# The third pass of a vision state-space, attention and FFN kernel: a list schedule, its residual stream spilled to DRAM, normalizations on ScalarE

## The chip, the cores and the metric

The kernel runs on one core of a Trainium2 chip. Time is device microseconds of one execution. Of the kernel before there are three runs: 10998.56, 11001.96 and 11004.07 us, median 11001.96. A separate execution was recorded by the hardware profiler; it took 11005.84 us, of which 11004.1 lie between its first and its last instruction (the span). Stages and lines below are of that execution.

The engines are PE (TensorE, the matmuls), DVE (VectorE), ACT (ScalarE), POOL (GpSimd) and SP, which here only issues DMA transfers. Each engine has a queue of its own and works it off strictly in the order in which the program was written down; an instruction whose inputs aren't ready holds up what stands behind it on that engine. PEld is PE's loading of weights.

## The reference

The input x is (8, 64, 64, 96) in f32: 8 images, 4096 tokens each, 96 channels. What is computed, cut to its core:

```python
# layer 0
x = x + L0_conv(gn(x))       # group norm, 96 -> 2 x 192 channels (xin, z), depthwise 3x3 conv, SiLU,
                             # a selective scan in four directions (16 states), y = their sum;
                             # y = layernorm_192(y) * gamma + beta; y = y * silu(z); out = y @ out_proj.T
# layer 1, per token t of 96 channels
t = t + L1_attn(ln_t(t))     # q, k, v = ln @ Wqkv + b, 6 heads of 16
                             # attn = q k^T * 16**-0.5 (no softmax), y = attn v, y @ Wff + bff
t = t + L1_ffn(ln_t(t))      # q_acc(q_mul(x) @ q_mul(W1).T + q_mul(b1)), relu, the same with W2: 96 -> 384 -> 96
# ln_t: (v - mean) / sqrt(var + 1e-5) over the 96 channels; q_mul rounds to 5 exponent and 2 mantissa bits
```

Attention without a softmax is linear: q (k^T v). So for one image it is enough to have the Gram matrix of its normalized tokens, 97x97 with a column of ones for the biases; from it follows one matrix of 97x96 that all the image's tokens are multiplied with.

## The kernel before

Three passes run one after the other over all images. The first makes the projections and the convolution, the second the scans, the third all that follows. The first two end at 9870 us of the profiled execution; the change leaves them as they are.

*The third pass.* An image is cut into 8 groups of 512 tokens (`UNITS`), a group into 4 blocks of 128 tokens (`NU`), tokens on the partitions. A **first half** (`first_part`) does this for one group: load y and yo, the sums of the two scan orientations, z and x (five transfers on SP); add y and yo on GpSimd; normalize y over its 192 channels; transpose it on PE into `pt` (two PSUM banks), scale and shift on ScalarE into `gt`; multiply with z on GpSimd; project on PE into `po`; add x on VectorE, which gives the residual stream `t`; normalize it into `ln`, with a column of ones; add its Gram matrix into `pg`, transpose it into `pl` and copy that to `lnT`. When 8 first halves of an image are done, `attention` makes the matrix `weff` out of `pg` in four small products. A **second half** (`second_part`) multiplies `lnT` with `weff` into `pa`, adds that to `t`, normalizes into `lf`, transposes (`pf`), rounds to 8-bit floats (`xq`), multiplies with W1 (three `ph`, copied to `h1` by ScalarE), adds the bias and clips on VectorE, rounds to `hq` on GpSimd, multiplies with W2 (`py`), copies to `y16`, adds the bias, adds to `t` on GpSimd and stores. With 8 images there are 64 first and 64 second halves; one of each is called a pair here.

*Normalizing.* `statistics` takes `bn_stats` and `bn_aggr` on VectorE and leaves mean and variance of 4 blocks in the small tile `mv`; `rstd_of` adds epsilon and raises to the power of -0.5 on GpSimd. Then y is normalized on ScalarE, after VectorE has made the bias -mean x rstd out of `mv` (`scalar_tensor_tensor`), and ln and lf on VectorE itself (`normalize`, one `tensor_scalar` per block):

```python
dve.tensor_scalar(dst[:, i, 0 : src.shape[2]], src[:, i, :], mv[:, i, 0:1], mv[:, i, 1:2], ALU.subtract, ALU.mult)
```

*Buffers.* `t` (12 KB a partition) and `lnT` (16 KB) hold a whole image each, in three buffers; what is loaded has five, most of the rest three or two. In PSUM there are three banks for transposes, two for products of 96 columns, two for `ph`, one for `pg`.

*The order.* Every half is a Python generator that yields between its steps. `take_turns` opens one unit in every second round, with at most 12 open, and in every round takes each open unit one step further. The list of units puts first halves of image b and second halves of image b-2 in alternation. So the order in which PE, VectorE, ScalarE and GpSimd find their instructions is that of the rounds, with no duration in it. `InOrder` keeps it on these four engines; the transfers on SP are ordered by the framework.

*The other way to order* is `weave`, which the first two passes use already. There a step yields an engine, a planned cost in us, a delay till its result can be used (0.3 where none is given), and if it needs a PSUM bank, that bank's `Slots`. `weave` keeps a planned time per engine and always writes down next the step that can begin earliest; among equals the one of smaller rank:

```python
begin = at[0] if len(at[5]) < 4 else max(at[0], at[5][3].when())
key = (max(begin, free.get(at[5][0], 0.0)), at[1])
if best is None or key < best[0]:
    best = key, at
```

A step that yields a name and numbers, such as `"weff", b`, waits for that event in the plan. `room` says how many units of a kind may be open at a time; the next opens when the one that many places before it has ended.

Of the kernel before, what the change touches and what calls it, by code (L numbers as in the profile page):

```python
# [33 lines left out]
F32 = mybir.dt.float32  # L34
F16 = mybir.dt.float16
BF16 = mybir.dt.bfloat16
F8 = mybir.dt.float8e5
AF = mybir.ActivationFunctionType
ALU = mybir.AluOpType
# [61 lines left out]
def vss_attn_ffn_kernel(ctx: ExitStack, tc: tile.TileContext, g: dict, out: bass.AP):  # L101
# [15 lines left out]

    b_d = [[dram.tile([2, NS, N, L], BF16, name=f"b_d{b}_{o}") for o in range(2)] for b in range(NB)]
# [6 lines left out]
    pass3(tc, g, ident, mhalf, engines, y_d, z_d, out)  # L125
# [705 lines left out]
def take_turns(units, every, at_most):  # L831

    active, rounds = [], 0
    units = iter(units)
    unit = next(units, None)
    while unit or active:
        if unit and rounds % every == 0 and len(active) < at_most:
            active.append(unit)
            unit = next(units, None)
        active = [u for u in active if next(u, "end") != "end"]  # L840
        rounds += 1


@with_exitstack
def pass3(ctx, tc, g, ident, mhalf, engines, y_d, z_d, out):
    nc = tc.nc
    pe, dve, act, pool = engines
    CA = C + 1
    wp = ctx.enter_context(tc.tile_pool(name="p3w", bufs=1))
    one = ctx.enter_context(tc.tile_pool(name="p3one", bufs=1))  # L850
    two = ctx.enter_context(tc.tile_pool(name="p3two", bufs=2))
    three = ctx.enter_context(tc.tile_pool(name="p3three", bufs=3))
    five = ctx.enter_context(tc.tile_pool(name="p3five", bufs=5))
    ps_tr = ctx.enter_context(tc.tile_pool(name="p3tr", bufs=3, space=PSUM))
    ps_mm = ctx.enter_context(tc.tile_pool(name="p3mm", bufs=2, space=PSUM))
# [40 lines left out]
    state = [{"units": 0} for _ in range(NB)]  # L896

    def statistics(src):

        st = three.tile([P, NU, 6], F32, name="st")  # L900
        mv = five.tile([P, NU, 2], F32, name="mv")
        for i in range(NU):
            dve.bn_stats(st[:, i, :], src[:, i, :])
        for i in range(NU):
            dve.bn_aggr(mv[:, i, :], st[:, i, :])
        return mv

    def rstd_of(mv):

        pool.tensor_scalar(mv[:, :, 1], mv[:, :, 1], 1e-5, None, ALU.add)  # L910
        pool.tensor_tensor(mv[:, :, 1], mv[:, :, 1], mhalf[:, 0:NU], ALU.pow)

    def normalize(dst, src, mv):
        for i in range(NU):
            dve.tensor_scalar(dst[:, i, 0 : src.shape[2]], src[:, i, :], mv[:, i, 0:1], mv[:, i, 1:2], ALU.subtract, ALU.mult)

    def tokens(src, q):
        return src[q * GRP : (q + 1) * GRP].rearrange("(n p) c -> p n c", p=P)

    def first_part(b, q):  # L920
        cols = slice(q * GRP, (q + 1) * GRP)
        if q == 0:
            state[b]["t"] = three.tile([P, NBLK, C], F32, name="t")
            state[b]["lnT"] = three.tile([CA, L], F32, name="lnT")
            state[b]["gram"] = ps_one.tile([CA, CA], F32, name="pg")
        t = state[b]["t"][:, NU * q : NU * (q + 1), :]
        lnT, pg = state[b]["lnT"][:, cols], state[b]["gram"]
        y, yo = (five.tile([P, NU, DI], F32, name=name) for name in ("y", "yo"))
        for o, dst in enumerate((y, yo)):
            nc.sync.dma_start(dst, tokens(y_d[b][o], q))  # L930
        zs = five.tile([P, 2, GRP], F32, name="zs")
        nc.sync.dma_start(zs[:, 0, :], z_d[b][0:P, cols])
        nc.sync.dma_start(zs[0 : DI - P, 1, :], z_d[b][P:DI, cols])
        xr = five.tile([P, NU, C], F32, name="xr")
        nc.sync.dma_start(xr, tokens(g["x"][b], q))
        for _ in range(3):
            yield
        pool.tensor_add(y, y, yo)
        yield
        mv = statistics(y)  # L940
        yield
        rstd_of(mv)
        yield

        dve.scalar_tensor_tensor(mv[:, :, 0], mv[:, :, 0], -1.0, mv[:, :, 1], ALU.mult, ALU.mult)
        yield
        for i in range(NU):
            act.activation(y[:, i, :], y[:, i, :], AF.Identity, bias=mv[:, i, 0:1], scale=mv[:, i, 1:2])
        yield
        pt = [ps_tr.tile([P, GRP], F32, name=f"pt{i}", tag="tr") for i in range(2)]  # L950
        for i in range(NU):
            blk = slice(i * P, (i + 1) * P)
            pe.transpose(pt[0][:, blk], y[:, i, 0:P], ident)
            pe.transpose(pt[1][0 : DI - P, blk], y[:, i, P:DI], ident)
        yield
        gt = three.tile([P, 2, GRP], F32, name="gt")
        for i, rows in enumerate((P, DI - P)):
            act.activation(gt[0:rows, i, :], pt[i][0:rows, :], AF.Identity, bias=gb[0:rows, i, 1:2], scale=gb[0:rows, i, 0:1])
        yield
        for i, rows in enumerate((P, DI - P)):  # L960
            pool.tensor_mul(gt[0:rows, i, :], gt[0:rows, i, :], zs[0:rows, i, :])
        yield
        po = ps_mm.tile([P, NU, C], F32, name="po", tag="mm")
# [4 lines left out]
        yield  # L968
        dve.tensor_add(t, po, xr)
        mv = statistics(t)  # L970
        yield
        rstd_of(mv)
        yield
        ln = three.tile([P, NU, CA], F32, name="ln")
        pool.memset(ln[:, :, C:CA], 1.0)
        normalize(ln, t, mv)
        yield
        pl = ps_tr.tile([P, GRP], F32, name="pl", tag="tr")
        for i in range(NU):
            at = NU * q + i  # L980
            pe.matmul(pg, ln[:, i, :], ln[:, i, :], start=at == 0, stop=at == NBLK - 1)
            pe.transpose(pl[0:CA, i * P : (i + 1) * P], ln[:, i, :], ident)
        yield
        act.copy(lnT, pl[0:CA, :])
        state[b]["units"] += 1

    def attention(b):

        def small(rows, lhsT, rhs, name):
            p = ps_mm.tile([P, NU, C], F32, name=f"ps_{name}", tag="mm")[0:rows, 0, :]  # L990
            pe.matmul(p, lhsT, rhs, start=True, stop=True)
            return p

        while state[b]["units"] < UNITS:
            yield
        yield
        gram = two.tile([CA, CA], F32, name="gram")
        dve.tensor_copy(gram, state[b]["gram"])
        yield
        p = small(CA, gram, w_kv[:, 1, :], "gv")  # L1000
        yield
        gv = two.tile([CA, C], F32, name="gv")
        dve.tensor_copy(gv, p)
        yield
        p = small(C, gv, w_kv[:, 0, :], "kvT")
        yield
        kvT = two.tile([C, C], F32, name="kvT")
        dve.tensor_mul(kvT, p, hmask)
        yield
        p = small(C, kvT, w_ff, "kvf")  # L1010
        yield
        kvf = two.tile([C, C], F32, name="kvf")
        dve.tensor_copy(kvf, p)
        yield
        p = small(CA, w_qT, kvf, "weff")
        yield
        weff = two.tile([CA, C], F32, name="weff")
        dve.tensor_copy(weff, p)
        dve.tensor_add(weff[C:CA, :], weff[C:CA, :], b_ff[C:CA, :])
        state[b]["weff"] = weff  # L1020

    def second_part(b, q):
        while "weff" not in state[b]:
            yield
        t = state[b]["t"][:, NU * q : NU * (q + 1), :]
        lnT = state[b]["lnT"]
        pa = ps_mm.tile([P, NU, C], F32, name="pa", tag="mm")
        for i in range(NU):
            blk = slice(q * GRP + i * P, q * GRP + (i + 1) * P)
            pe.matmul(pa[:, i, :], lnT[:, blk], state[b]["weff"], start=True, stop=True)  # L1030
        yield
        dve.tensor_add(t, t, pa)
        mv = statistics(t)
        yield
        rstd_of(mv)
        yield
        lf = three.tile([P, NU, C], F32, name="lf")
        normalize(lf, t, mv)
        yield

        pf = ps_tr.tile([P, GRP], F32, name="pf", tag="tr")
        for i in range(NU):
            pe.transpose(pf[0:C, i * P : (i + 1) * P], lf[:, i, :], ident)
        yield
        xq = two.tile([C, GRP], F8, name="xq")
        dve.tensor_copy(xq, pf[0:C, :], saturate=False)
        yield
        h1 = three.tile([P, NHC, GRP], F16, name="h1")
        for hc in range(NHC):
            ph = ps_mm.tile([P, GRP], F32, name="ph", tag="ph")  # L1050
            pe.matmul(ph, w1q[:, hc * P : (hc + 1) * P], xq, start=True, stop=True)
            act.copy(h1[:, hc, :], ph)
        yield
        for hc in range(NHC):
            dve.tensor_scalar(h1[:, hc, :], h1[:, hc, :], b1q[:, hc : hc + 1], 0.0, ALU.add, ALU.max)
        yield
        hq = two.tile([P, NHC, GRP], F8, name="hq")
        pool.tensor_copy(hq, h1, saturate=False)
        yield
        po = ps_mm.tile([P, NU, C], F32, name="py", tag="mm")  # L1060
# [3 lines left out]
        yield  # L1064
        y16 = two.tile([P, NU, C], F16, name="y16")
        act.copy(y16, po)
        yield
        dve.tensor_add(y16, y16, b2q.unsqueeze(1).to_broadcast([P, NU, C]))
        yield
        pool.tensor_add(t, t, y16)  # L1070
        nc.sync.dma_start(tokens(out[b], q), t)

    units = []
    for b in range(NB + 2):
        for q in range(UNITS):
            if b < NB:
                units.append(first_part(b, q))
            if b >= 2:
                units.append(second_part(b - 2, q))
        if b < NB:  # L1080
            units.append(attention(b))
    take_turns(units, 2, 12)
# [45 lines left out]
```

## Time and profile before

| | |
|---|---|
| median of 3 runs | 11001.96 us |
| the profiled execution | 11005.84 us, its span 11004.1 |
| last matmul of the second pass starts | 9866.5 us, 3.7 long |
| first GpSimd instruction of the third pass | 9893.0 us |
| first store of the output | 10052.2 us |
| last store of the output | 11000.9 us |
| busy in the whole span: PE, DVE, ACT, POOL | 7817.8, 9786.2, 9222.7, 9474.5 us |
| DMA: bytes, rate over the span | 2103.23 MB, 191 GB/s |

In a row of the profile a name stands for a tile with its buffer number left out, so `mv` is every such tile, and y and y16 are both `y`. "x256" counts instructions. Nearly all rows carry the line L91, the line of `InOrder` that records instructions, so they are told apart by their tiles. An f32 matmul is two records. A matmul's length in the profile is modelled, and matmuls overlap, so PE's busy time says little of how near it is to its peak. "Releaser" names what ended an engine's idle time; "issue" is time in which it waited for nothing that the profile shows.

### The profile page before, as it was taken

How to read it: one execution, taken by the hardware profiler on the slowest of the kernel's cores; microseconds unless marked ns; L12 is line 12 of the kernel's file. 1: busy time of each engine (PE TensorE's matmuls, PEld its weight loads, DVE VectorE, ACT ScalarE, POOL GpSimd, SP SyncE). 2: the span in 40 equal slices, each digit the busy share in tenths (PEclk: the TensorE clock that was granted, in tenths of full speed). 3: DMA queues.
4: the chain of work that ended last, by engine and by line, in shares of the span. 5: the costliest groups of instructions: out<-in, count | busy, mean ns of one | idle time of the engine just before them, and what ended most of it. 6: DMA issues, size and time to landing. Idle time of an engine off the chain costs nothing.

```text
span 11004.1 us, 151651 instructions
## 1 busy us (share of the span) xinstructions
PE 7817.8 (71%) x51232; PEld 6202.8 (56%) x51232; DVE 9786.2 (89%) x7286; ACT 9222.7 (84%) x21031; POOL 9474.5 (86%) x3366
## 2 busy tenths in 40 slices
PE   6874777777767777776677777776777777767667
PEld 2221656666556666665566666665666666556555
DVE  6671999999999999999999999999999999987777
ACT  4553999999999999999999999999999999973333
POOL 4563999999999999999999999999999999987555
PEclk8776999999899999989999999889999999887666
DMA  4554666669896666698966666989666668884331
GB/s 139 170 156 132 209 219 216 210 214 206 196 215 211 215 218 209 212 206 197 216 212 214 216 208 212 204 196 214 212 216 215 208 213 204 196 181 145 86 87 40
DMA packets 928011, 2103.23 MB, mean 191 GB/s; under 512 B 274392, under 2 KB 422649, under 8 KB 925701
## 3 DMA queue, kind: packets, MB, share of 16 engines
q1 hardware_dynamic: 927236, 2093.53, 67.6%
q8 instruction: 410, 6.72, 0.3%
q14 instruction: 365, 2.98, 0.1%
HBM read 1917.59 MB, written 175.66 MB: 190 GB/s over the span
## 4 chain that ended last, share of the span: by engine, by line
ACT 27%; DVE 21%; PE 17%; issue 17%; POOL 11%; DMA 2%; SPq 1%; DVEq 0%; POOLq 0%; ACTq 0%
DVE h L91 14%; ACT x L91 12%; ACT da L91 10%; POOL c L91 9%; PE wide L91 6%; PE acc L91 5%; DVE wide L91 3%; PE po L91 2%; DVE lf L91 2%; PE px L91 2%; ACT L91 1%; POOL xg L91 1%; PE pa L91 1%; ACT delta L91 1%; DVE ln L91 1%
## 5 line engine op out<-in xcount | busy, mean ns | idle before, releaser
L91 POOL TENSOR_TENSOR c<-c,h 128x2048 f32<-128x2048 f32 x1536 | 6965.3, 4547 | 394.8 <-DVE h L91 334.3
L91 DVE TENSOR_TENSOR_SCAN h<-da,carry,wide 128x1024 f32<-128x1024 f32 x2304 | 5253.1, 2330 | 199.6 <-PE wide L91 132.5
L91 ACT ACTIVATE x<-duT,bT 128x128 f32<-128x128 f32 (+1 forms) x14336 | 4154.9, 366 | 57.5 <-PE wide L91 51.2
L91 PE MATMUL acc<-ident,c 128*128 128x128 f32 x24576 | 3478.9, 297 | 548.6 <-POOL c L91 541.0
L91 ACT ACTIVATE da<-delta,a_neg 128x1024 f32<-128x1024 f32 x3072 | 3502.2, 1143 | 347.4 <-DVE h L91 336.5
L91 PEld LDWEIGHTS acc<-ident,c 128*128 128x128 f32 x24576 | 3129.5, 155 | 884.5 <-POOL c L91 750.9
L91 PE MATMUL wide<-ident,x 128*128 128x128 f32 x11264 | 1609.2, 291 | 874.1 <-DVE h L91 855.9
L91 PEld LDWEIGHTS wide<-ident,x 128*128 128x128 f32 x11264 | 1338.6, 149 | 1170.6 <-DVE h L91 512.5
L91 DVE TENSOR_TENSOR_SCAN h<-da,wide 128x1024 f32<-128x1024 f32 x768 | 1707.4, 2270 | 89.3 <-PE wide L91 61.1
L91 DVE TENSOR_TENSOR wide<-du,wide 128x1024 f32<-128x1024 f32 x1216 | 1458.7, 1211 | 335.0 <-DMA u<-u_d 224.1
L91 PE MATMUL wide<-xb,sel 96*128 96x512 bf16 x2432 | 751.7, 394 | 590.8 <-DVE h L91 495.2
L91 POOL TENSOR_TENSOR xg<-duT,bT 128x512 f32<-128x512 f32 (+1 forms) x640 | 890.9, 1406 | 77.5 <-PE wide L91 59.3
L91 PE MATMUL wide<-ident,xg 128*128 128x128 f32 x3584 | 503.4, 286 | 236.6 <-DVE h L91 231.2
L91 PEld LDWEIGHTS <-sel 96*128 96x128 bf16 x2432 | 222.9, 101 | 781.6 <-DVE h L91 387.6
L91 PEld LDWEIGHTS wide<-ident,xg 128*128 128x128 f32 x3584 | 415.2, 147 | 313.7 <-issue 147.2
L91 POOL TENSOR_TENSOR du<-delta,u 128x1024 f32<-128x1024 f32 x192 | 454.8, 2369 | 109.1 <-ACT delta L91 71.4
L91 ACT ACT_TABLE_LOAD x385 | 494.0, 1283 | 6.8
L91 PE MATMUL px<-u,w_xp 64*76 64x512 f32 (+1 forms) x512 | 402.6, 920 | 80.6 <-ACT xd L91 60.1
L91 DVE SCALAR_TENSOR_TENSOR u<-xpad,conv_w,u 128x3584 f32<-128x3584 f32 x96 | 423.6, 4413 | 1.6
L91 ACT ACTIVATE y<-y,mv 128x192 f32<-128x192 f32 x256 | 119.0, 536 | 338.3 <-DVE mv L91 294.6
L91 POOL TENSOR_TENSOR u<-u,term 128x512 f32<-128x512 f32 x96 | 286.7, 2986 | 130.7 <-ACT term L91 129.0
L91 POOL TENSOR_SCALAR mv<-mv 128x4 f32<-128x4 f32 x192 | 63.8, 332 | 382.5 <-DVE mv L91 381.7
(121 smaller groups left out, 6578.5 us busy)
## 6 DMA issues: line engine op xcount, KB each, us to landing
c<-xd_d SPq DMA_DIRECT2D x1024, 1024.0 KB
c<-xd_d SPq DMA_DIRECT2D x1024, 512.0 KB
u<-u_d SPq DMA_DIRECT2D x128, 512.0 KB
xdt<-dt_d SPq DMA_DIRECT2D x1152, 36.0 KB
xb<-b_d SPq DMA_DIRECT2D x384, 96.0 KB
u<-u_d SPq DMA_DIRECT2D x128, 256.0 KB
y_d<-y SPq DMA_DIRECT2D x24, 1024.0 KB
y<-y_d SPq DMA_DIRECT2D x64, 384.0 KB
```

The source lines that it names most:

```text
L91: ins = getattr(self.engine, op)(*args, **kwargs).ins
```

## The change

The third pass is written for `weave`; `take_turns` goes. Each step names its engine and a planned cost. At most 6 first halves, 1 attention and 6 second halves are open; the rank of a first half is 100 less than that of a second half of the same place, so among steps that can begin at the same time a first half's goes ahead.

`t` and `lnT` no longer stay in SBUF between the halves. A first half stores its 512 tokens of both in DRAM (`t_d`, `lnT_d`), and a second half loads them again. All tiles of the halves have six buffers. SP's transfers in this pass are held to the written order too.

All three normalizations go the way of y's: statistics on VectorE, power on GpSimd, bias on VectorE, and the last step on ScalarE. One of the three copies of `ph` to `h1` moves from ScalarE to VectorE. The two transposed halves of y take a bank each when they need it, and the Gram products of a group stand together ahead of its transposes. In the new queue of GpSimd 27 second halves have their last step before the last y plus yo, and 37 after it.

```diff
-    three = ctx.enter_context(tc.tile_pool(name="p3three", bufs=3))
-    five = ctx.enter_context(tc.tile_pool(name="p3five", bufs=5))
+    OPEN = 6
+    each = ctx.enter_context(tc.tile_pool(name="p3each", bufs=OPEN))
+    banks = {"tr": 3, "mm": 2, "ph": 2}
...
+    def standardize(src, dst, name, cost):
+        yield "dve", 4 * cost
         st = each.tile([P, NU, 6], F32, name=f"st{name}")
         mv = each.tile([P, NU, 2], F32, name=f"mv{name}")
...
+        yield "pool", 1.3
         pool.tensor_scalar(mv[:, :, 1], mv[:, :, 1], 1e-5, None, ALU.add)
         pool.tensor_tensor(mv[:, :, 1], mv[:, :, 1], mhalf[:, 0:NU], ALU.pow)
+        yield "dve", 0.15
+        dve.scalar_tensor_tensor(mv[:, :, 0], mv[:, :, 0], -1.0, mv[:, :, 1], ALU.mult, ALU.mult)
+        yield "act", 4 * cost
         for i in range(NU):
-            dve.tensor_scalar(dst[:, i, 0 : src.shape[2]], src[:, i, :], mv[:, i, 0:1], mv[:, i, 1:2], ALU.subtract, ALU.mult)
+            act.activation(dst[:, i, 0 : src.shape[2]], src[:, i, :], AF.Identity, bias=mv[:, i, 0:1], scale=mv[:, i, 1:2])
...
+        yield "pe", 3.8, 0.3, slots["mm"]
+        po, slot = take("mm", [P, NU, C])
...
+        end = yield "sp", 0.9, 3.0
+        sp.dma_start(tokens(t_d[b], q), t)
+        sp.dma_start(lnT_d[b][:, cols], lnT)
+        done["first", b, q] = end
...
     def second_part(b, q):
-        while "weff" not in state[b]:
-            yield
-        t = state[b]["t"][:, NU * q : NU * (q + 1), :]
-        lnT = state[b]["lnT"]
+        yield "first", b, q
+        yield "sp", 0.9, 3.0
+        t = each.tile([P, NU, C], F32, name="t2")
+        sp.dma_start(t, tokens(t_d[b], q))
+        lnT = each.tile([CA, GRP], F32, name="lnT2")
+        sp.dma_start(lnT, lnT_d[b][:, q * GRP : (q + 1) * GRP])
+        yield "weff", b
...
         for hc in range(NHC):
-            act.copy(h1[:, hc, :], ph)
+            end = yield ("act" if hc < 2 else "dve"), 0.6
+            (act.copy if hc < 2 else dve.tensor_copy)(h1[:, hc, :], ph)
...
-    take_turns(units, 2, 12)
+    for b in range(NB):
+        units += [("first", b * UNITS + q - 100, first_part(b, q)) for q in range(UNITS)]
+        units.append(("attention", 0, attention(b)))
+        units += [("second", b * UNITS + q, second_part(b, q)) for q in range(UNITS)]
+    weave(units, {"first": OPEN, "attention": 1, "second": OPEN}, done)
```

## The prediction

> **What bounds the kernel now.** I read the page's table of slices first, then busy time by stage, then the rows of the third pass, and last the order of time inside one of its periods. The change touches only the third pass, so the first question is how much that pass takes and how full its engines are. Slices of the page:
>
> ```profile
> DVE  6671999999999999999999999999999999987777
> POOL 4563999999999999999999999999999999987555
> PEclk8776999999899999989999999889999999887666
> ```
>
> Up to the 36th slice VectorE and GpSimd stand at nine tenths; after it both fall, and so does the clock. The last matmul of the second pass ends at 9870.2 us, the first instruction of the third pass on a compute engine other than weight casts (GpSimd, y plus yo) starts at 9893.0, the span ends at 11004.1. So the pass takes 1111 us after a gap of 23. The table of stages (columns: stretch, its length, busy us of PE, PEld, DVE, ACT, POOL with counts, clock, DMA share, GB/s):
>
> ```profile
> 9900.00:10000.00 100.00, 81.57 (x419) 65.84 (x417) 58.49 (x273) 46.84 (x89) 86.72 (x99) 0.70 0.72 210
> 10022.00:10898.00 876.00, 599.88 (x3091) 470.49 (x3091) 666.08 (x1969) 280.38 (x528) 514.65 (x579) 0.66 0.28 81
> 10898.00:11004.00 106.00, 74.87 (x455) 54.67 (x454) 90.38 (x283) 35.05 (x67) 62.54 (x64) 0.64 0.12 32
> ```
>
> At first only first halves run and GpSimd is 87% busy. In the 876 us in the middle, where a first and a second half alternate, nothing is full: VectorE 76%, PE 68%, GpSimd 59%. There the stores of the output lie 17.8 us apart (10052.2 to 10799.2, 42 intervals). At the end, second halves alone leave one per 5.95 us (10905.7 to 11000.9, 16 intervals). A first half among its like takes about 8 us even with the stalls of the start, so a pair costs more together than its halves apart. The next lines say why. Three are rows of groups (busy us, mean ns | idle us before); the fourth gives lf's shortest, median and longest ns; the last five are a stretch in order of time (start, length, and in brackets the idle time before):
>
> ```profile
> L91 DVE TENSOR_SCALAR lf<-t,mv 128x96 f32<-128x96 f32 x256 | 209.1, 879 | 1.4 <-POOL mv L91 1.3
> L91 DVE TENSOR_SCALAR ln<-t,mv 128x96 f32<-128x96 f32 x256 | 135.3, 590 | 9.7 <-POOL mv L91 9.4
> L91 DVE SCALAR_TENSOR_TENSOR mv<-mv 128x4 f32<-128x4 f32 x64 | 54.7, 855 | 4.8 <-POOL mv L91 4.8
> L91 DVE TENSOR_SCALAR lf<-t,mv x256: 291/325/4476, 10022.1 to 10990.1; 128x96 f32<-128x96 f32 x128
> ...
> 10503.91 6.28 DVE L91 TENSOR_SCALAR lf<-t,mv 128x96 f32<-128x96 f32 x4
> 10503.99 2.48 POOL L91 TENSOR_TENSOR gt<-gt,zs 128x512 f32<-128x512 f32 x2
> 10506.42 1.46 POOL L91 CAST hq<-h 128x1536 fp8e5<-128x1536 f16 x1
> 10507.84 1.79 POOL L91 TENSOR_TENSOR y<-y,yo 128x768 f32<-128x768 f32 x1
> 10509.76 0.64 PEld L91 LDWEIGHTS pf<-ident,lf 128*96 128x96 f32 x3 [4.27 <-DVE lf L91]
> ```
>
> A normalization instruction has a median of 325 ns but a mean of 879 (lf) and a longest of 4476: four of them take 6.28 us while GpSimd runs three kinds of work back to back, and PE waits 4.27 us for them. The chain of waits then alternates: DVE lf, PE po, DVE lf, PE po, through the whole pass. VectorE's 76% is thus partly standing still, and the written order puts PE's work behind it.
>
> [...] lf, ln and the two-input mv stretch, bn_stats with one input never does (240/243/263 ns shortest, median, longest). [...] the 4.4 us are longer than any one GpSimd instruction there, so back-to-back GpSimd work can keep VectorE out over several. [...] four pg and pl pairs took 2.3 us at the low clock and 1.15 at the high one; the mean clock of the pass is 0.66.
>
> **The change, part by part.** On every engine the instructions up to the end of the second pass stand in the same order, and the first loads of the third do too. So 9893.0 stays. Per pair of halves, 64 pairs:
>
> Removed from VectorE: lf and ln, (209.1 + 135.3)/64 = 5.4 us, of which some 2.5 is work (8 x 0.31) and 2.9 waiting. Added to it: two more mv of 0.15 (unblocked) to 0.86 (the mean of before); the third of the h1 copies, taken at 0.68 like the xq row of near size; together 1.0 to 2.4. VectorE's unblocked work is then 3.4 for a first half (bn_stats 1.86, bn_aggr 0.72, add 0.56, two mv 0.30) and 4.8 for a second (add 0.55, statistics 1.10, mv 0.15, xq 0.68, copy 0.68, three h1 1.05, y16 0.55): 8.2 a pair, 525 in all.
>
> Added to ScalarE: eight activations of 128x96. The rows of 128x64 (335 ns) and 128x128 (389) bracket them at 360: 2.9 us, less 0.59 for the h1 copy that leaves. ScalarE goes from 384/64 = 6.0 to 8.3 us a pair, 533 in all; it hides behind GpSimd. The normalization now goes VectorE, GpSimd, VectorE, ScalarE: one hop more, hidden by six open halves, and 0.5 us on the last unit only.
>
> GpSimd is unchanged: first half y 1.80, gt 2.54, two mv pairs 2.57, memset 0.13 = 7.04; second mv 1.29, hq 1.46, t 0.93 = 3.68. Together 10.7, 686 in all: the floor.
>
> PE's work is unchanged. From the first stage above: 419 records, 36 to a first half, so 11.6 halves in 81.6 us: 7.0 a half at clock 0.70. From the last: 74.9 us for 17.8 halves, 4.2 each.
>
> DMA: t and lnT are stored and loaded again, four transfers of 192 or 194 KB; a pair moves 2308 KB instead of 1536. SP issues 10 transfers a pair instead of 6, at 0.37 to 0.5 us each 4.5 us: hidden. Over some 820 us the 64 pairs make 151 MB, 184 GB/s; the stage of first halves already moved 210 at a DMA share of 0.72 with GpSimd fed. I take zero, covered by a pair's 10 to 13 us. Bound above: if the stage kept that 210, 720 us, still below my sum; late loads could add 100. A store of lnT waits for ScalarE, and behind it in SP's queue, now in written order, stand the loads for the half six later, some 60 us ahead: hidden.
>
> The order: in GpSimd's new queue 27 to 28 second halves stand among the 64 first halves, and about 36 follow the last. Stretch A, GpSimd: 64 x 7.04 + 28 x 3.68 = 554 us. At the 86.7% that the first-halves stage reached: 638. PE in it needs 64 x 7.0 + 28 x 4.2 = 566 at the clock of 0.70, VectorE 64 x 3.4 + 28 x 4.8 = 352 plus its blocks; three engines near each other, so I don't take more than 87%. Stretch B, 36 second halves: the 5.95 of before, less about 2.4 for lf (2.54, 1.86 and 2.80 in the tail), plus 0.68 and 0.5, gives 4.7; PE at the low clock needs 2.0 + 0.9 + 1.6 + 1.2 = 5.7. I take 5.2: 187. Draining the last half and its store, 10. Sum: 9893 + 638 + 187 + 10 = 10728 against the profiled span of 11004.1; the median of the runs is 2 us under that span, so **10726 us**, 2.5% faster.
>
> **Rivals.** *The order works better still.* The longer look-ahead fills GpSimd to 97% in A (571) and B runs at 4.7 (169): 10640. For it, the second pass, ordered by the same function, holds both engines at nine tenths; against it, PE's need beside a low clock. Chance 0.17.
>
> *Blocking or loads cost more.* A denser GpSimd blocks VectorE more often; seven instructions a pair (three mv, three h1, y16) can still be blocked. Means of before over their unblocked time: mv 0.70, lf 0.58, ln 0.28, h1 0.13, y16 0.03 us. At 0.75 each, VectorE needs 8.2 + 5.2 = 13.4 a pair, 64 x 13.4 = 860, with the same drain and some bubbles 10800 to 10900; late loads of t2 and lnT2 would give the same 10830. Chance 0.23.
>
> *Slower.* [...] VectorE in order stands behind each blocked mv, and ScalarE, PE and so GpSimd behind it. Before's period is 1111/64 = 17.36 us a pair. It decides from a mean wait of (17.36 - 8.2)/7 = 1.3 us per blockable instruction; with VectorE and GpSimd fully in turns, 8.2 + 10.7 = 18.9 a pair, the kernel ends near 9893 + 1210 = 11100. For it: single waits of 4.4 us exist already. Against it: the largest mean is 0.70, and a VectorE that lags starves GpSimd [...]. Chance 0.06, of which 0.01 falls within 0.2% of no change.
>
> *The list order does nothing:* the costs that it plans with are off (po is planned at 3.8 us and lasts 5.3 at the low clock, blocks at zero) and each queue's head waits, as in the turns. Only lf and ln's blocked 2.9 us a pair would be won at most, 186 us, and half given back to mv: about 10900 to 11000. Chance 0.04, of which 0.02 within 0.2%.
>
> **How the numbers follow.** My case, 10680 to 10800, has 0.50. Below it lies 0.17, above it 0.33. The range of 8 in 10 leaves out the best 0.08 and the worst 0.12: 10625 to 10905. A difference of under 0.2% (22 us) can hardly be told from no change. Faster by more: 0.92; within: 0.03; slower: 0.05.
>
> **What would show it.** Spans of the first two passes unchanged, first y plus yo at 9893. GpSimd at 80 to 90% from there for about 640 us, then 190 us of second halves at about 5.2 us apiece. No lf or ln on VectorE; 512 such activations on ScalarE of about 360 ns. The mean of mv on VectorE between 0.3 and 0.9 us; above 1.3 the slow rival holds. PE's clock in A above 0.70. DMA near 185 GB/s and no long waits for t2 or lnT2. I am wrong if the blocked instructions, or waits of GpSimd for PE or DMA, leave GpSimd under 75% in A.

## The result, and the profile after

The kernel after takes 11575.57 us (median of 4 runs, 11569.57 to 11581.51), the kernel before 11000.56 in the same comparison (4 runs, 10998.56 to 11004.07): ratio 1.0522, 95% interval 1.0504 to 1.0541. The change makes the kernel 575 us slower; the forecast was 10726. The profiled span is 11572.4 us. The first y plus yo of the third pass starts at 9894.4 us (9893.0 before), so everything was lost in the third pass: 1678 us instead of 1111.

The slices of the page after (same rows as shown of before, and the DMA share):

```profile
DVE  6663999999999999999999999999999999333334
POOL 4564999999999999999999999999999999444433
PEclk8766999998899999889999998999999989555555
DMA  4654666679976766889666678986666899433321
```

In the third pass the clock is down to five tenths, no engine but PE is half busy any more (PE, at that clock, 52% in A below), and the DMA engines, too, are mostly idle on average. No engine is full. The same by stretch, A from the first to the last y plus yo, B from there to the end (columns: stretch, its length, busy us of PE, PEld, DVE, ACT, POOL with counts, clock, DMA share, GB/s):

```profile
9893.00:11146.00 1253.00, 646.20 (x3112) 517.05 (x3112) 422.77 (x1726) 419.59 (x905) 534.32 (x618) 0.59 0.37 104
11146.00:11572.00 426.00, 181.71 (x984) 133.09 (x984) 169.35 (x566) 108.57 (x247) 144.32 (x150) 0.56 0.17 50
```

A lasts 1253 us where 638 were forecast, B with its draining 426 where 197 were. GpSimd does the 534 us of work in A that the sum of the prediction had put at 554, but is 43% busy with it instead of 87%. The waits of the third pass say what it waits for (us in total, times, longest), those of the compute engines:

```profile
POOL y L91 <- DMA yo<-y_d: 551.9, 53, 47.4
DVE sty L91 <- POOL y L91: 504.1, 48, 43.5
PEld mm L91 <- issue: 409.3, 334, 27.5
PE mm L91 <- DMA lnT<-lnT_d: 311.3, 41, 21.5
```

And those of SP's own queue in the same stretch:

```profile
SPq L91 <- DMA out<-t: 336.6, 57, 10.0
SPq L91 <- POOL t L91: 247.5, 35, 30.1
SPq L91 <- ACT lnT L91: 115.1, 15, 19.3
```

Transfers are late, although the rate is half of what it was in the first stage of before (104 against 210 GB/s). The place to look is where little else is under way, in B. One period of it in order of time (start, length; in brackets the idle time before and its releaser):

```profile
11438.02 1.99 PE L91 MATMUL mm<-weff,lnT 97*128 97x96 f32 x8 [7.93 <-DMA lnT<-lnT_d]
11438.74 0.36 SPq L91 DMA_DIRECT2D t<-t_d  x1
11439.15 0.35 SPq L91 DMA_DIRECT2D lnT<-lnT_d  x1
...
11444.39 0.38 SPq L91 DMA_DIRECT2D out<-t  x1
...
11449.41 1.57 PE L91 MATMUL mm<-weff,lnT 97*128 97x96 f32 x6 [4.83 <-DMA lnT<-lnT_d]
```

And the same period cut into short stretches, with the columns of the stages (the last two are the DMA share and GB/s):

```profile
11439.00:11441.00 2.00, 2.00 (x16) 1.72 (x16) 0.91 (x4) 0.52 (x1) 0.00 (x0) 0.50 0.41 104
11441.00:11442.50 1.50, 1.50 (x11) 0.96 (x8) 1.21 (x8) 0.55 (x2) 0.67 (x2) 0.54 0.10 26
11442.50:11444.20 1.70, 0.32 (x3) 0.11 (x2) 1.58 (x4) 0.00 (x0) 1.70 (x2) 1.00 0.06 25
11444.20:11446.00 1.80, 0.37 (x2) 0.00 (x0) 0.98 (x5) 1.39 (x4) 0.99 (x2) 0.94 0.43 126
11446.00:11447.50 1.50, 0.00 (x0) 0.00 (x0) 0.00 (x0) 1.50 (x6) 0.63 (x1) 0.50 0.07 27
11447.50:11449.20 1.70, 0.00 (x0) 0.00 (x0) 0.00 (x0) 1.16 (x4) 0.00 (x0) 0.50 0.07 25
```

A load of t and one of lnT, 192 and 194 KB, are issued within 0.5 us of each other. The load of t, and later the store of the output, show as short stretches at a share of 0.41 and 0.43. What remains for the rest of the time runs at a share of 0.06 to 0.07 and 25 to 27 GB/s: that is one of the sixteen DMA engines over which the page takes the mean (1/16 = 0.0625). The matmul that needs lnT starts 10.3 us after its load was issued. The packets in the trace agree: those of 2048 bytes, which in B are lnT's rows alone, follow one after the other, 84 ns each. 97 of them make 8.15 us; this load's took 8.05, since each starts 80 ns after the one before, with two short breaks. From 11280 to 11560 us exactly one was under way for 179 us, two for 9.

The store of the output that falls into this period shows what that does to a transfer that is spread. Of its 512 packets of 384 bytes, 480 ran from 11445.3 to 11446.1 us; the last 32, one sixteenth, began at 11448.97, right behind lnT's last packet, and were done at 11449.6. SP issued its next load at 11450.07.

lnT has 97 rows, 96 channels and the row of ones. Its packets went one by one (84 ns each, one every 80). Of the 512 packets of this load of t, four to a partition, up to 19 were under way at once, of those of the store up to 21. The measured share agrees: one engine works off lnT. That its 97 rows are the reason was the estimate to be tested.

From this the theory that the experiments test, called A: 64 stores and 64 loads of 97 rows take 128 x 8.15 = 1043 us of one engine, and every other transfer that is spread over all sixteen has a sixteenth of its bytes on that engine, and lands behind them. y and yo thus come late, and since SP issues strictly in order (all 5229 issues in the profile of after stand in the order of the program), so does what stands behind them. The rival B: it is the new queue of SP, where stores that wait for their data (247.5 and 115.1 us of SP's waits above) and loads of t2 that wait for a buffer (336.6) stand ahead of the loads of y, and six buffers of t2 and lnT2 are too few.

### The profile page after: what moved, and what is told of

Read it like the earlier page. It is cut to its first block, busy times and chain, and to the rows that moved or that the text cites. A ratio compares the mean times of both kernels' runs of the same rounds, so it can differ in the third digit from the quotient of the medians.

```text
span 11572.4 us, 152227 instructions
## 1 busy us (share of the span) xinstructions
PE 7870.1 (68%) x51232; PEld 6247.1 (54%) x51232; DVE 9545.3 (82%) x6966; ACT 9387.9 (81%) x21479; POOL 9471.1 (82%) x3366
## 4 chain that ended last, share of the span: by engine, by line
ACT 25%; DVE 17%; issue 16%; PE 14%; POOL 12%; DMA 8%; SPq 3%; DVEq 0%; POOLq 0%; ACTq 0%
DVE h L91 13%; ACT x L91 12%; ACT da L91 9%; POOL c L91 8%; PE wide L91 5%; PE acc L91 5%; DVE wide L91 3%; SPq L91 3%; DMA yo<-y_d 3%; PE mm L91 2%; DMA out<-t 2%; DMA lnT<-lnT_d 2%; PE px L91 1%; ACT L91 1%; POOL xg L91 1%
## 5 line engine op out<-in xcount | busy, mean ns | idle before, releaser
L91 POOL TENSOR_TENSOR y<-y,yo 128x768 f32<-128x768 f32 x64 | 115.4, 1804 | 607.0 <-DMA yo<-y_d 551.9
L91 DVE BATCH_NORM_STATS2 sty<-y 128x6 f32<-128x192 f32 x256 | 72.9, 348 | 576.3 <-POOL y L91 504.1
L91 ACT ACTIVATE y<-y,mvy 128x192 f32<-128x192 f32 x256 | 119.1, 539 | 371.8 <-DVE mvy L91 308.9
```

Source lines behind the costliest of these rows:

```text
L91: ins = getattr(self.engine, op)(*args, **kwargs).ins
```

## Experiments

All times are medians, beside runs of the kernel before on the same chip; ratios are to those, with 95% intervals.

**1. lnT as 96 rows and 1 row** (`e1_rows96`), otherwise the kernel after, the same for the load:

```diff
-        sp.dma_start(lnT_d[b][:, cols], lnT)
+        for rows in (slice(0, C), slice(C, CA)):
+            sp.dma_start(lnT_d[b][rows, cols], lnT[rows])
```

> The changed kernel, with each of the 128 transfers of lnT (97 rows of 2 KB) issued as two, 96 rows and 1 row; the same bytes, 128 more issues on SP. Theory A (a transfer of 97 rows is worked off by a single one of the 16 DMA engines, 97 packets of 84 ns one after the other = 8.15 us, 128 of them = 1043 us on that engine, and every other transfer has a share that stands behind them): 96 rows spread, about 0.5 us each, and the time falls to what was forecast for the change, 10650 to 10850 us. Theory B (SP's written order: the load of t2 waits for the output's store out of the same buffer to land, the store waits for GpSimd, and loads of y stand behind): nothing of that is touched, 11450 to 11650 us.

Measured 10857.34 us, ratio 0.9863 (0.9848 to 0.9877), 7 us above theory A's range and some 600 below theory B's. The same bytes in twice as many transfers take off 718 us. The waits of its third pass, the two lines that answer to those above:

```profile
POOL y L91 <- DMA yo<-y_d: 89.1, 26, 16.2
...
PE mm L91 <- DMA lnT<-lnT_d: 33.1, 21, 4.2
```

551.9 became 89.1, 311.3 became 33.1. SP's waits for its stores' data have not gone (POOL t 205.6, ACT lnT 175.2), only those for the landing of the output shrank, to 126.6. A holds: what is left of B in SP's queue can't be the main cause.

**2. More buffers instead** (`e2_more_buffers`): the kernel after, t2 and lnT2 with eight buffers, paid for by four of h1 and lf.

```diff
-        t = each.tile([P, NU, C], F32, name="t2")
+        t = more.tile([P, NU, C], F32, name="t2")
-        lnT = each.tile([CA, GRP], F32, name="lnT2")
+        lnT = more.tile([CA, GRP], F32, name="lnT2")
-        lf = each.tile([P, NU, C], F32, name="lf")
+        lf = less.tile([P, NU, C], F32, name="lf")
-        h1 = each.tile([P, NHC, GRP], F16, name="h1")
+        h1 = less.tile([P, NHC, GRP], F16, name="h1")
```

> The changed kernel with 8 instead of 6 buffers for t2 and lnT2 (and, to make room, 4 instead of 6 for h1 and lf), so that a load of t2 on SP waits for the landing of a store two halves further back. 97-row transfers stay. Theory A: the one DMA engine still needs 1043 us for lnT and some 64 x 6 = 390 us for its share of the rest, 1430 us from 9893 on: not under 11330 us, and I expect 11400 to 11570. Theory B: the 337 us that SP waits for stores to land go, and most of the loss with them: 10800 to 11200 us.

Measured 11452.87, ratio 1.0404 (1.0389 to 1.042), inside theory A's range. SP's waits for the landing of the output are no longer among its largest, and yet GpSimd waits as before:

```profile
POOL y L91 <- DMA yo<-y_d: 538.3, 56, 39.7
```

The buffers, less what the four of h1 and lf may cost, are worth 123 us beside the slow transfers; the 575 us they don't explain.

**3 and 4. The 97 rows in the kernel before** (`e3_before_97`, `e4_before_96`): two more stores of lnT per first half into DRAM that nobody reads, once with all 97 rows, once with 96. Nothing waits for them but the buffer.

The first:

```diff
         act.copy(lnT, pl[0:CA, :])
+        for i in range(2):
+            nc.sync.dma_start(lnT_d[b][i][:, cols], lnT)
```

The second:

```diff
         act.copy(lnT, pl[0:CA, :])
+        for i in range(2):
+            nc.sync.dma_start(lnT_d[b][i][0:C, cols], lnT[0:C])
```

> The kernel before with two more stores of lnT (97 rows of 2 KB) to DRAM in each first half, which nobody reads: the disputed transfers by themselves, 128 of them, on a kernel that has its own order and no spill otherwise. Theory A: the one engine needs 16.3 us a first half for them and about 4.7 for its share of the rest, 21 us against a period of 17.4 and of 8 where first halves run alone: 11200 to 11400 us. Theory B: 24.8 MB more in 1111 us and two issues of 0.4 us on an SP that is mostly idle: 10990 to 11030 us.

> As the run with 97 rows on the kernel before, but the two stores of each first half take only the first 96 rows of lnT (the row of ones is left out; nobody reads either). Theory A: 6 rows to each of 16 engines, 1 us a first half together: 10990 to 11030 us. If the number of bytes or of issues is what costs, it is as slow as the one with 97 rows.

Measured 11259.19, ratio 1.0225 (1.0208 to 1.0242), with 97 rows, and 11007.77, ratio 1.0005 (0.9996 to 1.0013), with 96. One row more costs 251 us; 128 stores of 192 KB cost nothing that can be measured. The first stage of the third pass with 97 rows:

```profile
9900.00:10000.00 100.00, 57.18 (x263) 46.58 (x264) 33.83 (x177) 27.48 (x52) 54.42 (x62) 0.59 0.46 129
```

And with 96 rows:

```profile
9900.00:10000.00 100.00, 83.07 (x438) 66.70 (x438) 58.98 (x281) 47.87 (x92) 87.95 (x101) 0.75 0.80 230
```

With more bytes than before (230 GB/s instead of 210) GpSimd is as busy as before, 88%. With 97 rows it falls to 54%, in the old order and with no spilled tile to be loaded. This is the effect of the slow transfers alone.

**5 and 6. What each part is worth once that is out of the way.** `e5_before_act`: the kernel before, its turns kept, only ln and lf normalized on ScalarE. `e6_rows96_dve`: the kernel of experiment 1 with ln and lf back on VectorE, so the list order, the spill and the moved copy of h1 without the normalizations.

The first of the two:

```diff
     def normalize(dst, src, mv):
+        dve.scalar_tensor_tensor(mv[:, :, 0], mv[:, :, 0], -1.0, mv[:, :, 1], ALU.mult, ALU.mult)
-            dve.tensor_scalar(dst[:, i, 0 : src.shape[2]], src[:, i, :], mv[:, i, 0:1], mv[:, i, 1:2], ALU.subtract, ALU.mult)
+            act.activation(dst[:, i, 0 : src.shape[2]], src[:, i, :], AF.Identity, bias=mv[:, i, 0:1], scale=mv[:, i, 1:2])
```

The second:

```diff
         pool.tensor_tensor(mv[:, :, 1], mv[:, :, 1], mhalf[:, 0:NU], ALU.pow)
+        if name != "y":
+            yield "dve", 1.1
+            for i in range(NU):
+                dve.tensor_scalar(dst[:, i, 0 : src.shape[2]], src[:, i, :], mv[:, i, 0:1], mv[:, i, 1:2], ALU.subtract, ALU.mult)
+            return
```

> The kernel before with one part of the change alone: ln and lf normalized on ScalarE (with a bias made on VectorE), everything else, the turns too, as before. Theory P (the blocked normalizations on VectorE set the period): the 4 to 6 us that lf holds up PE and VectorE in each 17.8 us go, 10700 to 10900 us. Theory Q ([...] each mv instruction stands right behind GpSimd's power in time, finds GpSimd at its next work, and waits as lf did): 10950 to 11050 us.

> The changed kernel with lnT moved as 96 and 1 rows, and ln and lf back on VectorE (planned at 1.1 us each), y still on ScalarE: what the move of the normalizations is worth within the new order. Theory P: VectorE gets 5 to 8 us a pair back, blocked time included, and becomes the bound: 10930 to 11050 us. Theory Q: [...] 10830 to 10900 us, near the 10857 of that kernel with them on ScalarE.

Measured 10855.13, ratio 0.9865 (0.985 to 0.9879), and 10921.92, ratio 0.9926 (0.9912 to 0.9941). The first lies in theory P's range; the second lies between the two ranges, 22 us above Q's and 8 below P's. The normalizations alone bring 149 us, as much as experiment 1 (146). Order, spill and moved copy alone bring some 80; with the normalizations there, they add nothing in the form of experiment 1 (10857.34 against 10855.13). The two gains don't add up. The rows of the moved instruction in the third pass of the first of the two:

```profile
L91 ACT ACTIVATE ln<-t,mv 128x96 f32<-128x96 f32 x256 | 98.5, 460 | 33.9 <-DVE mv L91 33.9
L91 ACT ACTIVATE lf<-t,mv 128x96 f32<-128x96 f32 x256 | 98.2, 460 | 30.0 <-DVE mv L91 30.0
```

**7 and 8. SP's queue after all, as a second-order cost.** `e7_rows96_more`: experiments 1 and 2 together. `e8_rows96_act_stores`: experiment 1 with the stores of t and lnT issued by ScalarE, where they hold up no load. The diff of the second:

```diff
-        end = yield "sp", 0.9, 3.0
-        sp.dma_start(tokens(t_d[b], q), t)
+        end = yield "act", 0.3, 3.0
+        act.dma_start(tokens(t_d[b], q), t)
         for rows in (slice(0, C), slice(C, CA)):
-            sp.dma_start(lnT_d[b][rows, cols], lnT[rows])
+            act.dma_start(lnT_d[b][rows, cols], lnT[rows])
```

> The changed kernel with lnT moved as 96 and 1 rows and 8 buffers for t2 and lnT2 (4 for h1 and lf): what SP's waits for the landing of output stores (127 us in 55 waits with 6 buffers) still cost. If they delay loads that engines wait for (GpSimd 89 us for yo, PE 33 us for lnT): 10770 to 10830 us. If SP's waits are slack: 10840 to 10875 us.

> The changed kernel with lnT moved as 96 and 1 rows and the stores of t and lnT issued by ScalarE right behind its copy of lnT, instead of by SP, so that no load stands behind SP's wait for that copy (175 us in 28 waits). If these waits delay loads that engines wait for: 10760 to 10830 us. If they are slack, or ScalarE's three issues a half cost as much: 10840 to 10900 us.

Measured 10815.39, ratio 0.9828 (0.9813 to 0.9842), and 10870.55, ratio 0.9878 (0.9862 to 0.9895). The buffers are worth 42 us, and SP's waits for the landing of the output are no longer among its largest. Taking the stores of t and lnT off SP brought nothing (13 us more, the intervals overlap); whether SP's waits for lnT, 175 us in sum, are slack, or ScalarE's own issues took back what they cost, no run separates. So B exists, but small: 42 us here and 123 in experiment 2, against 718 for A.

**9 to 11. The 130 us between experiment 1 and the forecast.** In its first 700 us PE is 81% busy at a clock of 0.69, GpSimd 74%:

```profile
9900.00:10600.00 700.00, 565.76 (x2948) 457.09 (x2948) 428.46 (x1656) 399.31 (x868) 517.32 (x600) 0.69 0.64 174
```

`e10_one_product` leaves out the second of the two products into po (so the last 64 of 192 channels are not projected), `e11_no_gate` leaves out the product with z on GpSimd; both are the kernel of experiment 1 otherwise. `e12_measured_costs` takes experiment 7 and plans with the durations that its rows show. Without the product:

```diff
-            pe.matmul(po[:, i, :], gt[:, 0, blk], w_out0, start=True, stop=False)
-            pe.matmul(po[:, i, :], gt[0 : DI - P, 1, blk], w_out1, start=False, stop=True)
+            pe.matmul(po[:, i, :], gt[:, 0, blk], w_out0, start=True, stop=True)
```

Without the gate:

```diff
             yield "pool", 1.3
-            pool.tensor_mul(gt[0:rows, i, :], gt[0:rows, i, :], zs[0:rows, i, :])
```

With measured costs, two of some fifteen:

```diff
-        yield "pe", 3.8, 0.3, slots["mm"]
+        yield "pe", 5.6, 0.3, slots["mm"]
...
-        yield "dve", 0.15
+        yield "dve", 0.7
```

> The kernel after with lnT moved as 96 + 1 rows, and the second of the two products of a block into po (the last 64 of the 192 channels) left out: 8 of 16 records of PE for each first half, the rest and its order unchanged. At the mean of 0.38 us a record in its rows that is 64 x 8 x 0.38 = 195 us of PE work less. Theory E (PE at its low clock is what fills the time while first halves run: 82 to 89% busy there, GpSimd 69 to 80%): at least half of it comes off 10857, 10660 to 10760. Theory G (GpSimd remains the bound, PE only waits along with it): 10820 to 10860. Theory L (neither; late landings and the order in the queues set the pace): 10820 to 10860.

> The kernel after with lnT moved as 96 + 1 rows, and the product of gt with zs left out (GpSimd, 2.54 us for each first half, 163 us in all; zs is still loaded and not read). Theory G (GpSimd is the bound while first halves run): 10690 to 10750. Theory E (PE is): 10800 to 10860, since GpSimd had 20 to 30% to spare. Theory L: 10800 to 10860 too; it is told from E by the run with one product left out.

> The kernel after with lnT moved as 96 + 1 rows, eight buffers for t2 and lnT2 and four for h1 and lf (10815), and the planned costs of the third pass set to the durations that its rows show: po 5.6 instead of 3.8, pt 1.4 instead of 0.6, pg 2.5 instead of 1.6, pl and pf 1.35 instead of 0.7, pa 2.6 instead of 1.3, py 2.0 instead of 1.0, mv 0.7 instead of 0.15, statistics and activations up by a seventh to a quarter. If an order made from wrong costs is what keeps the kernel from the forecast of 10726: 10700 to 10770. If PE's work at the low clock is the bound whatever the order: 10790 to 10840.

Measured 10819.37 (0.9827, 0.9812 to 0.9842) without the product, 10807.0 (0.982, 0.9805 to 0.9835) without the gate, 11023.9 (1.0018, 1.0011 to 1.0024) with measured costs. PE's busy time fell by 168 us (755 to 588 from 9900 on) and brought 38; GpSimd's fell by 162 (676 to 514) and brought 50. Theory E had asked for 10660 to 10760 without the product, theory G for 10690 to 10750 without the gate: neither engine is the bound by itself. Two stages of the run without the product show GpSimd full in one and starved in another, while PE has time to spare in both:

```profile
10200.00:10300.00 100.00, 60.31 (x432) 53.57 (x432) 78.16 (x285) 68.92 (x154) 89.07 (x105) 0.77 0.69 188
...
10400.00:10500.00 100.00, 59.78 (x359) 45.57 (x360) 57.64 (x212) 47.96 (x106) 64.63 (x71) 0.65 0.56 154
```

The miss is the run with measured costs: truer costs make the order worse by 209 us, against both expectations. Its stretch A lasts 922 us where experiment 7 has 720 (first to last y plus yo), for the same number of second halves to within two; GpSimd waits for yo 165.0 us instead of 66.6. In the order that these costs give, the loads are late again. Why wasn't settled; what the run shows is how much the order hangs on the planned numbers.

**12. Planning the landing later** (`e13_landing`): experiment 7, and the data of the two loads of a half planned to be there 9 us after the issue instead of 3.

```diff
-        yield "sp", 2.4, 3.0
+        yield "sp", 2.4, 9.0
...
-        yield "sp", 0.9, 3.0
+        yield "sp", 0.9, 9.0
```

> The kernel after with lnT moved as 96 + 1 rows, eight buffers for t2 and lnT2 and four for h1 and lf (10815), and one planned number changed at the two loads: their data is planned to be there 9 us after the issue instead of 3. Theory L (what is left of the forecast lies in loads that the written order uses too early; GpSimd waits 66.6 us for yo there): the waits for yo shrink to under 35 us and the time to 10700 to 10790. Theory E+G (PE and GpSimd hold each other up at 84 to 90% and 72 to 83%, whatever the loads do): 10800 to 10840. If the order gets worse by being planned anew, as with the durations of the rows: above 10840.

Measured 10795.0 us, ratio 0.9817 (0.9801 to 0.9834), the lowest median of this study. The wait of GpSimd for yo in experiment 7:

```profile
POOL y L91 <- DMA yo<-y_d: 66.6, 24, 10.7
```

With the landing planned later:

```profile
POOL y L91 <- DMA yo<-y_d: 21.1, 8, 6.0
```

The wait shrinks as expected; the time lies between the two expectations. The gain is not sure: it is 20 us between the medians, but the kernel before beside this run took 10994.81 instead of 11003.86, and the ratio's interval overlaps that of experiment 7. In the profiled executions the third pass, from its first y plus yo on, lasts 900 us instead of 928. Late loads were at most a small part of the rest.

## Why the prediction was wrong

**The step that failed is the DMA term**: "I take zero, covered by a pair's 10 to 13 us. Bound above: if the stage kept that 210, 720 us, still below my sum; late loads could add 100." It was worked out as bytes by rate. Neither bytes nor rate were the problem: experiment 1 moves the same bytes, at 174 GB/s in its first 700 us. What counts is how a transfer is spread: 97 rows stand on one engine for some 8 us, where a sixteenth of 194 KB per engine would be some six rows, 0.5 us at 84 ns a packet (an estimate). The term measured 718 us (11575.57 less 10857.34) in place of 0 to 100. The row count stood in the diff, `[CA, GRP]` with CA = 97. The third pass of before moves no such tile, but its first pass held a warning: 128 stores of xd with 76 rows of 2 KB. While these run, from 213 to 933 us, exactly four packets of 2 KB were under way for 144 us, longer than any other number but none. One such store that stands alone, at 224.4 us, took 2.1 us and had four of its 76 packets under way at once for 1.4 us of them, never more than five.

**The second failing step is the lead of the loads**: "behind it in SP's queue ... stand the loads for the half six later, some 60 us ahead: hidden". They were never that far ahead, with or without the 97 rows. From the issue of yo's load to the y plus yo that reads it, the median over the 64 halves is 78.7 us in before, 10.8 after (longest 11.9) and 6.3 in experiment 1 (longest 11.6). In the chain of work that ended last (start, length) such a load looks like this after:

```profile
10509.48 10.40 DMA yo<-y_d
```

And in experiment 1:

```profile
10558.47 6.24 DMA yo<-y_d
```

Six open halves are thus no look-ahead of six halves for the loads. The runs show two things that shorten the lead: `weave` was told that a load needs 3 us (told 9, experiment 12, the median is 10.9), and stores stand ahead on SP (issued by ScalarE, experiment 8, it is 10.3). So there was little to hide a late transfer behind. How much of the 718 us lies in this short lead, and how much in the second halves that wait for lnT itself, no run separates; in the kernel before, where no engine waits for what they write, 128 such stores cost 251.

The late landings come on top. SP itself was held up in y's own issues, a median of 3.0 us each (ns shortest, median, longest; y and yo are the first transfers of a half):

```profile
L91 SPq DMA_DIRECT2D y<-y_d x63: 367/3019/8424, 9897.2 to 11129.5; - x63
```

In the third pass of before the same row reads:

```profile
L930 SPq DMA_DIRECT2D y<-y_d x63: 359/360/1485, 9895.8 to 10794.5; - x63
```

With 96 and 1 rows the median is 377 ns. There the short lead costs less, but it isn't hidden either: GpSimd still waits 89.1 us for yo (experiment 1).

**What held** (figures of the run after). 9893 as the start: 9894.4. GpSimd's floor of 686 us: 678.6 in the pass. The copy of h1 on VectorE: 682 ns for 680. The price of mv: 829, 470 and 414 ns in mvt, mvy and mvf, inside the bracket of 0.15 to 0.86 and far from the 1.3 us at which the slow rival decides; so by that sign it was not GpSimd holding up VectorE that made the kernel slow. The blocking itself is in the profile of before: the 55 lf with no GpSimd instruction beside them took at most 328 ns; 91 of the 256 took over one and a half times the median of 325, and GpSimd was at work in 92% or more of the time of each. The bias and clip of h1, which also reads one tensor, took over one and a half times its median of 350 in 34 of 192 cases, at most 1831 ns, while bn_stats, with GpSimd beside it 119 times, stayed within 263. Why the ones and not the other, no run shows. The condition named as proof of error, GpSimd under 75% in A, is what the profile showed: 43%. The rival with late loads named the right kind of cause and gave it some 100 us (10830), on the faster side of before.

**What was off beside that.** The activation takes 460 ns, not 360. The rows that I bracketed it with multiply by a scale alone. The row of y, 128x192 with a scale and a bias, 536 ns, stood in the same profile; less 96 columns at 0.84 ns, the slope of those two rows, it gives 455. No run shows that this cost time. The four pg and pl pairs, in the profile of before, take 2.36 us at a clock of 0.50 (at 10512.1 us) and 1.34 at 1.00 (at 10909.4), not 1.15. With lnT mended, A lasts 747 us (9890.8 to 10637.4) instead of 638, and B 226 with its draining instead of 197. "I don't take more than 87%" was still too high for GpSimd, since in experiment 1 it is 74% busy beside a PE of 81%; experiments 9 and 10 show that less work on either alone gives back less than a third of it (38 of 168, 50 of 162). And the gain was put down to the wrong part: the rival "the list order does nothing" gave the normalizations alone 10900 to 11000; alone they reach 10855.13, as much as both together in experiment 1. The cause of the 69 us that still lie between 10795.0 and 10726 stays open.

## What to carry to other kernels

Cost a transfer by its shape before its bytes. Here 97 rows of 2 KB took 8.05 us with one packet of 84 ns behind the other, 76 such rows 2.1 us with four at once, and 97 rows in place of 96 cost the kernel before 251 us. So look at the row count, read in a trace how many packets of such a transfer are under way at once, and multiply the time of a packet by the rows that fall on one engine. The 97 rows that a row of ones makes out of 96 were mended with a second transfer of that one row. The sign in this profile was a DMA share near 0.06 while someone waited for a landing: one engine of sixteen is busy, and what is spread over all of them lands behind it, while the average looks idle. And when a load counts as hidden, measure how long before its use it is issued: open buffers alone don't say it.

## What the runs showed of the hardware that was not expected

- A load of 97 rows of 2 KB took 8.05 us in the period shown, one packet of 84 ns behind the other at a DMA share of one sixteenth, and a store that is spread over all engines got its last sixteenth only behind it (from 11448.97 us on, where the rest was done by 11446.1). Two such stores per first half, unread, cost the kernel before 2.25%; the same two with 96 rows 0.05%, not distinguishable from nothing.
- With the 97-row transfers an issue on SP took longer: y's median was 3019 ns, against 360 before and 377 with 96 + 1 rows.
- A ScalarE activation of 128x96 from SBUF to SBUF with a scale and a bias per partition took 460 ns in the mean (ln and lf in experiment 5, 256 of each).
- PE's granted clock was lower where the transfers were late: 0.59 in A with the 97 rows, 0.69 in the first 700 us of experiment 1, 0.73 in those of experiment 12; in the first stage of the kernel before 0.59 with the 97-row stores and 0.75 with 96 rows (experiments 3 and 4). So late transfers came with a slower PE as well.
